# Reordering the first transfers of a two-layer graph network: x of three groups and the 1x1 weights on one queue, the taps' first quarter behind them on two

## The chip, the cores and the metric

The kernel runs on one core of one Trainium2 chip. A core has five engines that run their own instruction streams in order and meet through semaphores: TensorE (PE, matrix products), VectorE (DVE), ScalarE (ACT), GpSimd (POOL) and SyncE (SP, which here does nothing but issue transfers). Transfers (DMAs) can be issued from SyncE, ScalarE and GpSimd; "queue" below means the stream of transfers that one of these engines issues. The metric is the device time of one launch in microseconds; for several runs the median is given.

## The reference

There are 128 graphs of 128 nodes with 256 channels. The part that the change touches is the beginning of layer 0:

```python
h = jnp.maximum(_layernorm(x, axis=-1), 0.0)
...
xc = jnp.transpose(x, (0, 2, 1))          # x is h here
h = _bn(_conv1d(xc, conv1_w, 0), bn1_g, bn1_b, bn1_m, bn1_v)
h = jax.nn.relu(h)
h = _bn(_conv1d(h, conv2_w, 8), bn2_g, bn2_b, bn2_m, bn2_v)
x_conv = jnp.transpose(jax.nn.relu(h + xc), (0, 2, 1))
```

So x is normalized row by row, goes through a 1x1 convolution (`conv1_w`, 256 by 256), a batch norm and a relu, and then through a convolution of 17 taps (`conv2_w`). The rest of layer 0 (an attention-like neighbour product and a gated recurrent unit) and layer 1 (graph convolutions over five groups of nodes) come later and are not touched.

## The kernel before

**Tiles and stages.** x is handled in 32 groups of 4 graphs. Group q sits in the tile `xa` (128 partitions, 4 x 256 values, 512 KB), which has four buffers. `load_x` (lines 357 to 360) fills it with four transfers of 128 KB, each into 32 partitions, all issued from SyncE. `moments` (L267 to L270) takes mean and variance on VectorE and raises the variance to the power -1/2 on GpSimd; `normalize` (L275, VectorE) applies them.

`stage_a` (L367 to L418) then takes a group through PE: transposes to `ph` (L386), a relu to `hTa` on ScalarE (L388), a write of `hTa` to memory from GpSimd (L391), the 1x1 convolution to `pc` (L397), bias and relu to `h` (`h1` in the code; L400 on VectorE, L402 on ScalarE), and a Fourier transform over nodes to `pf` (L408), which is copied to X (L414 or L416). Sixteen groups make a batch; `stage_b` multiplies their spectra by the transformed taps, frequency by frequency.

**The taps.** The taps' transform is made once, beside `stage_a` of the first batch, in four quarters. `load_taps(n, *engines)` (L426 to L433) loads quarter n into one of two buffers of `wt`: four transfers of 256 KB, each into 16 partitions, with transfer r on `engines[r % len(engines)]`, and one of 64 KB (the seventeenth row of each block, L432) on `engines[0]`. `tap_weights` (L435) multiplies them on PE (`pw`, L450), copies the results to `ws` (two buffers; L455, L457) and writes these to memory as `wfd` from GpSimd (L462). Quarters 1 to 3 are loaded from inside `tap_weights` (L441), from SyncE and GpSimd; quarter 0 is loaded ahead of everything.

**Order.** Within one engine, instructions run in the order in which the program states them. That order is made by `Order` and `Lane` (L156 to L204), which interleave the stages by stated costs; it does not depend on how fast transfers are. Ahead of it stands an opening written out by hand (L1099 to L1106): the constants (`cst`, L229) and vectors (`vec`, L231) are issued from ScalarE, then x of group 0, the 1x1 weights `c1w`, x of group 1, the taps' first quarter, x of group 2, and `fold()`.

`fold` (L278 to L302) folds the batch norms into scales: a power on GpSimd (L286), the statistics of group 0 (L287, through `moments`), small VectorE operations (L289 to L291), eight products on PE that spread the scales over columns (`prow`, L297), the normalization of group 0 (L298), and the multiplication of `c1w` by the scales (L301). Then the planned order starts with `stage_a` of three groups at once. On VectorE that puts the statistics of groups 1 and 2 ahead of L400 of group 0, and the statistics of group 3 right before the first tap products are drained.

The opening, as it is before the change:

```python
take_turn("ab", 2)
load_xa(0)
nc.scalar.dma_start(out=c1w, in_=conv1_w.rearrange("(k p) o -> p k o", p=P))
load_xa(1)
load_taps(0, nc.sync, nc.gpsimd, nc.scalar)
load_xa(2)
fold()
```

With three engines given, tap transfers 0 and 3 and the 64 KB one are SyncE's, 1 is GpSimd's and 2 is ScalarE's.

Of the kernel before, what the change touches and what calls it, by code (L numbers as in the profile page):

```python
# [19 lines left out]
P = 128  # L20
# [187 lines left out]
def kernel(ctx: ExitStack, tc: tile.TileContext, x, adj, consts, vecs, w_se, conv1_w,  # L208
                    conv2_w, w_msg, b_msg, w_ih, w_hh, W1, W2, b2, fusion_w, out):
    nc = tc.nc  # L210
# [22 lines left out]
    def c(name):  # L233
        a, b = CAT[name]
        return cst[:, a:b]

    def v(name, i=None):
        a, b = VAT[name]
        return vec[:, a:b] if i is None else vec[:, a + i:a + i + 1]
# [21 lines left out]
    def moments(src, tag):  # L261

        st = f2.tile([P, 4, 6], FP, tag=tag + "st", name="st", bufs=4)
        mv = f2.tile([P, 4, 2], FP, tag=tag + "mv", name="mv", bufs=4)
        rs = f2.tile([P, 4], FP, tag=tag + "rs", name="rs", bufs=4)
        for t in range(4):
            nc.vector.bn_stats(st[:, t], src[:, t])  # L267
            nc.vector.bn_aggr(mv[:, t], st[:, t])
        nc.vector.tensor_scalar(rs, mv[:, :, 1], EPS, None, op0=ALU.add)
        nc.gpsimd.tensor_tensor(rs, rs, c("mhalf")[:, :4], ALU.pow)  # L270
        return mv, rs

    def normalize(dst, src, mv, rs):
        for t in range(4):
            nc.vector.tensor_scalar(dst[:, t], src[:, t], mv[:, t, 0:1], rs[:, t:t + 1],  # L275
                                    op0=ALU.subtract, op1=ALU.mult)

    def fold():  # L278


        s = cp.tile([P, 4], FP, name="s_bn")
        t = cp.tile([P, 4], FP, name="t_bn")
        for i, bn in enumerate(("bn1", "bn2")):
            scl[bn], sft[bn] = s[:, 2 * i:2 * i + 2], t[:, 2 * i:2 * i + 2]
            nc.vector.tensor_scalar(scl[bn], v(bn + "_v"), EPS, None, op0=ALU.add)
        nc.gpsimd.tensor_tensor(s, s, c("mhalf")[:, :4], ALU.pow)  # L286
        MOM[0] = moments(XA[0], "a")  # L287
        for bn in ("bn1", "bn2"):
            nc.vector.tensor_mul(scl[bn], scl[bn], v(bn + "_g"))  # L289
            nc.vector.tensor_mul(sft[bn], v(bn + "_m"), scl[bn])  # L290
            nc.vector.tensor_sub(sft[bn], v(bn + "_b"), sft[bn])  # L291
        prow = ptmp.tile([P, 4, P], FP, tag="tmp", name="prow")
        wide = tw.tile([P, 4, P], FP, tag="wide", name="wide", bufs=1)
        for i, a in enumerate((scl["bn1"][:, 0:1], scl["bn1"][:, 1:2], sft["bn1"][:, 0:1],
                               sft["bn1"][:, 1:2])):
            nc.vector.tensor_copy(wide[:, i], a.to_broadcast([P, P]))
            nc.tensor.matmul(prow[:, i], wide[:, i], ident, start=True, stop=True)  # L297
        normalize(XA[0], XA[0], *MOM[0])  # L298
        nc.vector.tensor_add(brz, v("b_ih")[:, 0:4], v("b_hh")[:, 0:4])
        for k in range(2):  # L300
            nc.vector.tensor_mul(c1w[:, k], c1w[:, k], prow[:, 0:2].rearrange("p a c -> p (a c)"))  # L301
        nc.vector.tensor_copy(brow, prow[:, 2:4].rearrange("p a c -> p (a c)"))  # L302
# [42 lines left out]
    c1w = xf.tile([P, 2, D], FP, name="c1w")  # L345
# [16 lines left out]
    def load_xa(q):  # L362
        if q not in XA:
            XA[q] = LATE["ab"].tile([P, 4, D], FP, tag="xa", name=f"xa{q}", bufs=4)
            load_x(XA[q], q)
# [60 lines left out]
    def load_taps(n, *engines):  # L426

        wt = tw.tile([P, 16, D], FP, tag="wt", name=f"wt{n}")
        src = conv2_w.rearrange("(r n i) t o -> n t r i o", r=4, n=4)[n]
        for r in range(4):  # L430
            engines[r % len(engines)].dma_start(out=wt[32 * r:32 * r + 16], in_=src[:16, r])
        engines[0].dma_start(out=wt[16::32], in_=src[16])  # L432
        wts.append(wt)  # L433
# [665 lines left out]
    order = Order()  # L1099
    take_turn("ab", 2)  # L1100
    load_xa(0)
    nc.scalar.dma_start(out=c1w, in_=conv1_w.rearrange("(k p) o -> p k o", p=P))
    load_xa(1)
    load_taps(0, nc.sync, nc.gpsimd, nc.scalar)
    load_xa(2)
    fold()  # L1106
    beside = Lane([tap_weights()] + [early(q) for q in range(NQ)])
    gates = Lane([fold_gates()], weight=0.5)
# [61 lines left out]
```

## Time and profile before

| What | Value |
|---|---|
| median of three runs | 2103.17 us (2101.92 to 2105.74) |
| the profiled execution | 2104.03 us |
| its span, first to last instruction | 2102.1 us |
| PE busy | 2046.5 us (97%) |
| DVE, POOL, ACT busy | 1180.4 (56%), 723.3 (34%), 687.3 (33%) |
| DMA, first six of 40 slices (52.5 us each) | share 0.9, 0.9, 0.9, 0.7, 0.7, 0.7 |
| moved in these slices | 178, 269, 271, 235, 246, 265 GB/s |
| first matmul | 15.20 us after the span's start |
| first product with taps (L450) | 36.76 us |
| PE busy in 0 to 190 us | 160.84 us |

All times inside an execution are counted from the start of its span. The 1.9 us between the span and the execution's time lie around the first and last instruction. The page's share of busy time is an average over stages, so the opening, one and a half per cent of the span, does not show in it; views cut to the first tens of microseconds do: the chain of waits (what each step was released by, followed back from the end), the timeline, the waits of one engine, and tables of busy time by stretches. A row of such a table has the stretch, its length, busy time of PE, PEld (the loading of weights into PE), DVE, ACT and POOL with the instructions in brackets, PE's granted clock, the DMA share (time that packets took, over 16 engines; it can exceed 1, since packets overlap) and GB/s.

### The profile page before, as it was taken

The numbers are of one execution on the slowest core, as the hardware profiler recorded it, in microseconds if no ns is written. First come the engines' busy times: TensorE is split into PE (matmuls) and PEld (weight loads), VectorE is DVE, ScalarE is ACT, GpSimd is POOL, SyncE is SP. The second block draws the span as 40 slices with busy tenths as digits, with TensorE's granted clock in tenths as the row PEclk, the third lists the DMA queues.
The fourth block names the chain that finished last, engine by engine and source line by source line (L and its number), as shares of the span: only waits on it lengthen the run. The fifth ranks groups of instructions, "written<-read, shape, count | busy, mean of one in ns | idle before, by whom it ended". The sixth has DMA issues, their size and how long they took to land.

```text
span 2102.1 us, 31046 instructions
## 1 busy us (share of the span) xinstructions
PE 2046.5 (97%) x11316; PEld 1656.8 (79%) x11316; DVE 1180.4 (56%) x2775; ACT 687.3 (33%) x1543; POOL 723.3 (34%) x900
## 2 busy tenths in 40 slices
PE   6999999999999999999999999999999999999998
PEld 4667888789888788787778877878787787778875
DVE  5665444786544455645654664566465655654642
ACT  3554222344222333323232232232233323223333
POOL 2443566232565222503332233224323323233230
PEclk9999999999999999999999999999999999999999
DMA  9997778744777634222323332323232333223121
GB/s 178 269 271 235 246 265 263 211 154 151 247 259 258 203 111 141 75 78 73 89 78 86 88 84 71 91 72 87 78 94 73 79 92 92 79 81 99 34 75 51
DMA packets 187050, 281.66 MB, mean 134 GB/s; under 512 B 20685, under 2 KB 140242, under 8 KB 186898
## 3 DMA queue, kind: packets, MB, share of 16 engines
q1 hardware_dynamic: 156066, 184.81, 30.8%
q0 software_dynamic: 30000, 94.13, 13.9%
q8 instruction: 90, 1.47, 0.3%
q10 hardware_dynamic: 832, 0.74, 0.2%
q14 instruction: 62, 0.51, 0.1%
HBM read 187.34 MB, written 92.27 MB: 133 GB/s over the span
## 4 chain that ended last, share of the span: by engine, by line
PE 91%; DMA 3%; DVE 3%; issue 1%; POOL 1%; ACT 0%; SPq 0%; POOLq 0%; DVEq 0%; ACTq 0%
PE p L708 42%; PE pa L501 7%; PE pm L600 5%; PE ph L1030 5%; PE pz L1039 5%; PE pc L397 4%; PE pb L501 3%; PE pi L673 3%; PE px L626 3%; PE pf L408 2%; DMA wfd<-ws 2%; PE pg L1073 1%; PE pc L687 1%; PE po L854 1%; PE ph L386 1%; PE py L1013 1%
## 5 line engine op out<-in xcount | busy, mean ns | idle before, releaser
L834 POOL TENSOR_TENSOR d<-hTc,r 128x512 f32<-128x512 f32 x64 | 81.4, 1273 | 374.1 <-ACT r L831 374.1
L501 PE MATMUL pa<-wf,X 128*128 128x256 f32 x640 | 152.4, 381 | 0.0
L863 POOL DMA_DIRECT2D out<-xt x128 | 71.9, 567 | 206.8 <-DVE xt L860 204.0
L524 DVE SCALAR_TENSOR_TENSOR y<-pa,kk 128x512 f32<-128x512 f32 x78 | 53.8, 690 | 147.4 <-ACT kk L523 147.4
L723 ACT ACTIVATE z<-z,brz 128x256 f32<-128x256 f32 x128 | 58.1, 501 | 225.1 <-DVE z L780 190.9
L708 PE MATMUL p<-th,wrz 128*128 128x256 f32 x512 | 131.6, 379 | 0.0
L708 PE MATMUL p<-tc,wrz 128*128 128x256 f32 x512 | 131.5, 379 | 0.0
L708 PE MATMUL p<-tm,wrz 128*128 128x256 f32 x512 | 131.4, 379 | 0.0
L501 PEld LDWEIGHTS pa<-wf,X 128*128 128x128 f32 x640 | 118.1, 190 | 16.4 <-issue 2.2
L397 PE MATMUL pc<-c1w,hTa 128*128 128x256 f32 x512 | 122.4, 385 | 3.5 <-ACT ef L588 2.3
L600 PE MATMUL pm<-wmsg,hT 128*128 128x256 f32 x512 | 121.7, 382 | 0.0
L690 DVE SCALAR_TENSOR_TENSOR xc<-pc,s_bn,hTc 128x256 f32<-128x256 f32 x128 | 53.1, 476 | 117.4 <-PE pc L687 117.4
L397 PEld LDWEIGHTS pc<-c1w,hTa 128*128 128x128 f32 x512 | 94.1, 192 | 21.6 <-DVE h L400 4.0
L1030 PE MATMUL ph<-yz,w 128*128 128x96 f32 (+3 forms) x640 | 109.0, 324 | 0.9 <-DVE yz L1015 0.9
L600 PEld LDWEIGHTS pm<-wmsg,hT 128*128 128x128 f32 x512 | 95.6, 190 | 16.0 <-issue 1.4
L1032 ACT ACTIVATE hh<-ph,vec 128x96 f32<-128x96 f32 (+3 forms) x160 | 64.2, 403 | 134.0 <-PE ph L1030 124.5
L708 PEld LDWEIGHTS p<-tm,wrz 128*128 128x128 f32 x512 | 97.3, 190 | 13.2
L1039 PE MATMUL pz<-hh,w 128*128 128x96 f32 (+3 forms) x640 | 107.3, 321 | 0.0
L1030 PEld LDWEIGHTS ph<-yz,w 128*128 128x128 f32 x640 | 87.9, 192 | 22.0 <-issue 15.6
L708 PEld LDWEIGHTS p<-tc,wrz 128*128 128x128 f32 x512 | 95.0, 190 | 12.1 <-issue 0.5
L708 PEld LDWEIGHTS p<-th,wrz 128*128 128x128 f32 x512 | 94.7, 190 | 12.3 <-DVE fus L895 0.3
L708 PE MATMUL p<-hTc,wrz 128*128 128x256 f32 x384 | 103.7, 393 | 0.0
(203 smaller groups left out, 4568.8 us busy)
## 6 DMA issues: line engine op xcount, KB each, us to landing
wf<-wfd SPq DMA_DIRECT2D x160, 256.0 KB, 3.9
wfd<-ws POOLq DMA_DIRECT2D x64, 320.0 KB, 7.0
yd<-y POOLq DMA_DIRECT2D x80, 256.0 KB, 3.7
yt<-yd SPq DMA_DIRECT2D x64, 320.0 KB, 4.5
w<-in_W SPq DMA_DIRECT2D x40, 512.0 KB, 3.6
xa<-in_x SPq DMA_DIRECT2D x128, 128.0 KB, 4.9
hTd<-hTa POOLq DMA_DIRECT2D x32, 512.0 KB, 4.6
hT<-hTd SPq DMA_DIRECT2D x32, 512.0 KB
```

What stands on the lines that cost most here:

```text
L397: nc.tensor.matmul(pc[:, i], hT[:, k, (2 * h + i) * N:(2 * h + i + 1) * N], c1w[:, k], start=(k == 0), stop=(k == 1))
L501: nc.tensor.matmul(ps, xk(k), WF[f][:, k, s], start=(k == 0), stop=(k == 1))
L600: nc.tensor.matmul(pm[:, i], hT[:, k, j * N:(j + 1) * N], LATE["wmsg"][:, k], start=(k == 0), stop=(k == 1))
L626: nc.tensor.matmul(px[:, dc, i], msgs[h][:, i, dc * P:(dc + 1) * P], aT[:, 2 * h + i], start=True, stop=True)
L673: nc.tensor.matmul(pi[b * 64:(b + 1) * 64], inv[:F], yt[:, b::2], start=True, stop=True)
L708: nc.tensor.matmul(ps[:, m], w[:, i, k, m * P:(m + 1) * P], factor(i, x, t), start=first and j == 0, stop=last and j == len(n) - 1, skip_g ...
L723: nc.scalar.activation(dst[:, m], src[:, m], AF.Sigmoid, bias=brz[:, b + m:b + m + 1])
L834: nc.gpsimd.tensor_sub(d, hT[:, dc], r[:, dc])
L863: nc.gpsimd.dma_start(out=out[q * GB + j, WIDE:].rearrange("(t n) c -> n t c", n=WIDE), in_=xt[j * WIDE:(j + 1) * WIDE, 1:4])
L1030: nc.tensor.matmul(ph, w1[:, k, m * P:(m + 1) * P], yz[:, k, :, o:o + n], start=(k == 0), stop=(k == 1))
L1032: nc.scalar.activation(hh[:, m], ph, AF.Relu, bias=v("b1", g * 4 + m))
L1039: nc.tensor.matmul(pz, w2[:, g, m, cc * P:(cc + 1) * P], hs[g][:, m], start=(m == 0), stop=(m == 3))
```

## The change

The 1x1 weights are issued from SyncE in place of ScalarE, at the same place among the x loads. The call that loads the taps' first quarter leaves the opening and goes into `fold`, behind the statistics of group 0, and is given two engines: tap transfers 0 and 2 and the 64 KB one are now GpSimd's, 1 and 3 are SyncE's.

```diff
@@ fold()
         nc.gpsimd.tensor_tensor(s, s, c("mhalf")[:, :4], ALU.pow)
         MOM[0] = moments(XA[0], "a")
+        load_taps(0, nc.gpsimd, nc.sync)
         for bn in ("bn1", "bn2"):
@@ the opening
     take_turn("ab", 2)
     load_xa(0)
-    nc.scalar.dma_start(out=c1w, in_=conv1_w.rearrange("(k p) o -> p k o", p=P))
+    nc.sync.dma_start(out=c1w, in_=conv1_w.rearrange("(k p) o -> p k o", p=P))
     load_xa(1)
-    load_taps(0, nc.sync, nc.gpsimd, nc.scalar)
     load_xa(2)
     fold()
```

SyncE's order is thus: group 0 (four transfers), `c1w`, group 1 (four), group 2 (four), taps 1 and 3, and then the x of group 3, which `stage_a` asks for. On GpSimd the three tap issues stand behind the power of L270 for group 0 and ahead of the one for group 1. ScalarE issues nothing more after the constants and vectors. The order of all other instructions on every engine is the same.

## The prediction

> **What bounds the kernel now.** The page's first part has PE busy 97% of the span, so a change at the start matters only if PE is held up there. The chain of waits, cut to 10 to 38 us, shows that it is:
>
> ```profile
> 2.11 9.40 DMA xa<-in_x
> ...
> 15.20 2.08 PE prow L297 x8
> 17.27 1.71 PE ph L386 x8
> 18.98 4.38 PE pc L397 x16
> 23.36 3.77 issue
> 27.13 2.25 PE ph L386 x8
> ```
>
> Columns: start, length, what. Read two holes. PE does nothing until 15.20, because group 0 of x lands at 2.11 + 9.40 = 11.51. Then it stops from 23.36 to 27.13. The chain calls that "issue"; the timeline of 23 to 27.5 us tells more:
>
> ```profile
> 23.69 0.43 DVE L267 BATCH_NORM_STATS2 st<-xa 128x6 f32<-128x256 f32 x1 [2.96 <-DMA xa<-in_x]
> ...
> 25.95 0.17 DVE L269 TENSOR_SCALAR rs<-mv 128x4 f32<-128x4 f32 x1
> 26.03 0.68 DVE L400 TENSOR_TENSOR h<-pc,brow 128x512 f32<-128x512 f32 x1
> ...
> 26.63 1.05 DVE L275 TENSOR_SCALAR xa<-xa,mv,rs 128x256 f32<-128x256 f32 x3
> ```
>
> VectorE executes in order. The statistics of group 2 stand ahead of h (L400) of group 0 and of the normalization (L275) of group 1, which PE's next transposes need. They wait 2.96 us for group 2, which lands at about 23.6. So both holes are late x. Why it is late shows in SyncE's own waits, 0 to 30 us (total, times, longest):
>
> ```profile
> SPq L359 <- DMA c1w<-in_conv_w: 4.6, 1, 4.6
> ...
> SPq L359 <- DMA wt<-in_conv_w: 4.1, 3, 1.7
> SPq L359 <- DMA cst<-in_consts: 2.0, 1, 2.0
> SPq L359 <- DMA vec<-in_vecs: 1.3, 1, 1.3
> ```
>
> An x load waits for the landing of c1w, of taps, of constants: none is its data. It is a limited number of hardware transfers in flight (eight stand issued when SyncE first stops, at 2.56), so what is issued early holds back what follows. The table by stretches has the rate in its last column (the share of DMA time is before it):
>
> ```profile
> 2.50:3.50 1.00, 0.00 (x0) 0.00 (x0) 0.00 (x0) 0.84 (x1) 0.00 (x0) 1.00 1.09 351
> 3.50:7.00 3.50, 0.00 (x0) 0.00 (x0) 0.24 (x2) 0.44 (x1) 0.05 (x1) 1.00 1.01 126
> 7.00:9.00 2.00, 0.00 (x0) 0.00 (x0) 0.00 (x0) 0.00 (x0) 0.98 (x1) 1.00 1.15 230
> 9.00:11.00 2.00, 0.00 (x0) 0.00 (x0) 0.00 (x0) 0.00 (x0) 0.00 (x0) 1.00 1.18 97
> ...
> 21.00:26.00 5.00, 2.35 (x11) 1.71 (x10) 2.13 (x9) 0.00 (x0) 0.82 (x1) 1.00 1.09 214
> 26.00:27.80 1.80, 0.67 (x3) 0.39 (x3) 1.80 (x6) 0.63 (x1) 1.60 (x2) 0.87 0.20 46
> ...
> 40.00:46.00 6.00, 6.00 (x38) 3.53 (x37) 3.97 (x9) 3.05 (x7) 3.22 (x6) 1.00 0.63 188
> ```
>
> With taps in flight the engines are taken up yet move 97 to 131 GB/s (131 in 14 to 19 us); in 21 to 26 us, nearly all x, they move 214. Lastly, does time won at the start last? From 190 us on, PE is busy in 1885.66 of 1912 us, so a shift reaches the end. From 30 to 190 us transfers are dense and PE also waits for ws buffers that writes to wfd still read; there a shift could be given back.
>
> **What the Trainium skill says.** "DMA: Bandwidth & Descriptors", section "Issuing engines are not separate DMA queues": transfers from all issuers share 16 DMA engines; another issuer saves only issue time. So moving c1w from ScalarE to SyncE brings no bandwidth; only the order counts. The trace agrees: the waits above cross queues. "SBUF — State Buffer", section "Door 1: The DMA port swizzle": a transfer's bandwidth depends on how many of 16 ports its partitions reach. By its table one tap transfer (16 partitions) reaches 4, an x transfer (32) reaches 8. The trace agrees in direction (97 to 131 against 214 GB/s), without showing ports. "TensorE: Matmul & The Clock Gate", Part 1: an idle window of about 3.4 us halves the clock. Here 27.8 to 29.6 us has a granted clock of 0.50, after the 3.77 us hole.
>
> **The change, part by part.** L marks the landing of group 0.
>
> 1. Removed from the opening: one tap transfer on GpSimd (issued 1.33), one on ScalarE (2.14); c1w now stands behind group 0 on SyncE. Ahead of L remain constants 188 KB, vectors 24.5 KB, group 0 512 KB: 742 kB. First packets move at about 1.7 us; at 214 GB/s that takes 3.5 us, so 5.2. Another estimate: the last of four issues ends at 2.56, and the x load issued at 29.4 into a nearly empty system landed 2.4 us after its issue. I take L = 5.5. Bounds: 4.8 (the second estimate), and 7.6 (742 kB at 126 GB/s). Gain at L: 11.51 - 5.5 = 6.0.
>
> 2. Group 2 moves ahead of three tap issues on SyncE and behind c1w (one issue, 0.46 us). Bytes up to group 2: 742 + 262 + 1049 = 2053 kB, landing 1.7 + 9.6 = 11.3; at the 167 GB/s that 2 to 27 us averaged, 14.0. VectorE gets to group 2 after group 1: group 1's statistics began 18.32 - 11.51 = 6.8 after L and take 2.4, thus L + 9.2 = 14.7. Group 2 is there in both cases and its wait goes. What is late next is VectorE's own chain: 2.34 us (23.69 to 26.03) of statistics, so L400 starts at L + 11.5 = 17.0 instead of 26.03. Shift there: 9.0 us (6.0 from L, 3.0 from group 2). PE's transposes of group 1 follow at 18.1 instead of 27.13, and the hole shrinks to L + 12.6 less the end of pc at L + 11.85, under 1 us. Clock: the cold stretch may go, yet after 27.13 VectorE sets the pace (L275, then L400 at 29.21), so I count nothing for it.
>
> 3. c1w: landed at 1.65 + 9.9 = 11.55, used by L301 at 17.31 = L + 5.8. Afterwards landed at 1.7 + 1004/214 = 6.4, used at 11.3: hidden, by the statistics. ScalarE loses two issues (0.46 + 0.49), and it is idle until 18.16: nothing.
>
> 4. GpSimd issues three tap transfers (0.69 us was the one at 1.33; about 2 us) behind the power of group 0, which ended at 15.18 = L + 3.7, so 9.2 to 11.2. Behind them waits the power of group 1 (L270), whose input comes at L + 9.2 = 14.7: hidden by 3.5 us; uncovered it would cost 2. hTd of group 0 comes later still.
>
> 5. Taps land later than before in relation to PE. Their first product stood at 36.76, now 27.8; group 3's statistics at 36.61, now 27.6. After group 2 (11.3) there are 1.11 MB of taps and 0.52 MB of group 3 to move: at 146 GB/s (between the 131 and 161 of 14 to 19 and 19 to 21 us) until 22.5. By the longest landing of any tap transfer, 14.0 us, counted from 10.4: 24.4. Hidden by 3 to 5 us.
>
> 6. Backlog. Before, everything up to group 4 (4.17 MB in 2 to 27 us) was in when PE resumed at 27. Now, at 18.1, about 2.05 + 6.8 us x 150 GB/s = 3.1 MB are in; 1.1 MB, or 5.2 us at 214, run into later traffic. Idle DMA time can absorb it: 1.4 us in 26 to 27.8 (share 0.20), 0.7 in 29.6 to 30.4 (share 0.07), 2.2 in 40 to 46 (share 0.63), 4.3 in all. I charge 1.0 us; bounds 0 and 5.2.
>
> Sum: 9.0 - 1.0 = 8.0 us. The profiled execution took 2104.03 (span 2102.1, 1.9 around it): 2096.0. The median of the runs shown, 2103.17, is 0.9 below it: 2095.2.
>
> **Rivals.** (a) The backlog isn't absorbed: the waits for wfd writes, already 3.9 us of PE at 79.8 to 83.65, grow by up to 5.2. For: 60 to 80 us has a DMA share of 1.03. Against: 0.63 in 40 to 46 shows that queues drain. Gain 9.0 - 5.2 = 3.8: 2099.4. (b) More: L = 4.8, no charge, and a cold window fewer at one later wait, where PE works at half speed for 3.4 us, worth 1.7. Gain 9.7 + 1.7 = 11.4: 2091.8. (c) The change doesn't do what it says: the opening is slow by itself, not through taps, and group 0 still lands near 11. For: 97 GB/s at 9 to 11 us with c1w and x in flight too. Against: 351 GB/s at 2.5 to 3.5 before taps piled up. Then group 2 still comes earlier, but behind c1w; gain 0 to 2: 2102. (d) Slower: taps on GpSimd, issued 8 us later, land after PE wants them; PE is in order, so everything behind L450 waits. It costs from 27.8 on, and the kernel is slower from 36.8, 26 us after issue where 14.0 was the longest. Landing at 41: + 4.2, 2107.4.
>
> **How the numbers follow.** Main case 0.60 (2093 to 2098), (a) 0.19, (b) 0.10, (c) 0.05, (d) 0.06. Range 2091 to 2101: it leaves out (c), (d), and the ends of (a) and (b). 0.2%, about what can be told from no change, is 4.2 us, so faster means below 2099.0: main, (b) and a third of (a), 0.76; same: the rest of (a) and (c), 0.18; slower 0.06.
>
> **What would show it.** Group 0's first L267 near 5.6 (now 11.64), L400's first near 17, PE's idle time ahead of group 1's transposes under 1 us, no wait for taps at the first L450 near 28, and the same distance still there at 190 us, where the chain turns to PE. I am wrong if L267 starts after 8, if PE waits at L450, or if the shift of 9 us near 27 has shrunk below 5 by 190.

## The result and the profile after

| | before | after |
|---|---|---|
| median of 20 runs each | 2104.34 us (2101.11 to 2112.02) | 2096.78 us (2094.63 to 2103.97) |
| profiled execution, its span | 2104.03, 2102.1 us | 2096.45, 2094.4 us |
| PE busy | 2046.5 us | 2042.4 us |
| group 0 of x lands | 11.51 us | 6.39 us |
| first h of group 0 (L400, now L401) | 26.03 us | 17.95 us |
| transposes of group 1 on PE | 27.13 us | 19.06 us |
| first product with taps | 36.76 us | 28.68 us |

The ratio is 0.9965, with an interval of 0.9957 to 0.9973: faster, by 7.6 us between the medians and 7.6 us between the profiled executions. From line 288 to the opening the line numbers are one higher than before.

First the chain of waits of the kernel after, cut to 0 to 26 us (start, length, what):

```profile
2.11 4.28 DMA xa<-in_x
...
10.07 2.09 PE prow L298 x8
...
18.05 0.59 DVE h L401
18.64 2.58 DVE xa L275 x8
...
23.02 2.05 PE pc L398 x8
```

The first wait is for the same transfer as before, the last of group 0, but 4.28 us long in place of 9.40: L, the landing of group 0, is 2.11 + 4.28 = 6.39. `prow` moves with it. The piece of "issue" of 3.77 us is gone; in its place the chain runs through VectorE, from h of group 0 to the normalization of group 1.

The timeline of the kernel after, cut to the instructions that the forecast named (start, length, engine, line, operation; in brackets the idle time before it):

```profile
6.51 0.43 DVE L267 BATCH_NORM_STATS2 st<-xa 128x6 f32<-128x256 f32 x1 [0.95 <-DMA xa<-in_x]
...
15.61 0.43 DVE L267 BATCH_NORM_STATS2 st<-xa 128x6 f32<-128x256 f32 x1
15.69 1.03 POOL L270 TENSOR_TENSOR rs<-rs,cst 128x4 f32<-128x4 f32 x1 [3.75 <-DVE rs L269]
...
17.95 0.68 DVE L401 TENSOR_TENSOR h<-pc,brow 128x512 f32<-128x512 f32 x1
...
19.06 1.69 PE L387 MATMUL ph<-cst,xa 128*128 128x128 f32 x8 [0.55 <-PE pc L398]
...
28.68 1.10 PE L451 MATMUL pw<-wt,cst 17*80 17x512 f32 x8
```

The line at 15.61 is group 2. It has no bracket: VectorE goes straight from group 1's statistics to group 2's, where it stood 2.96 us before. GpSimd has idled 3.75 us when the power of group 1 comes up, so the tap issues that now stand ahead of it (9.99 to 11.94) were done in time. PE's hole ahead of the transposes of group 1 is 0.55 us. The first product with taps has no bracket either: the taps are there.

SyncE's waits of the kernel after, 0 to 30 us (total, times, longest):

```profile
SPq L360 <- DMA xa<-in_x: 4.3, 5, 3.2
...
SPq L360 <- DMA wt<-in_conv_w: 1.5, 1, 1.5
...
SPq L360 <- DMA c1w<-in_conv_w: 0.6, 1, 0.6
```

The wait of an x load for c1w has shrunk from 4.6 to 0.6 us, those for taps from 4.1 to 1.5. What is left are mostly waits of x for earlier x, and for the release of a buffer of x (3.7 us for PE, 3.4 for VectorE; not shown).

And the table by stretches of the kernel after (DMA share and GB/s are the last two columns):

```profile
2.50:3.50 1.00, 0.00 (x0) 0.00 (x0) 0.00 (x0) 0.44 (x1) 0.00 (x0) 1.00 1.06 329
3.50:7.00 3.50, 0.00 (x0) 0.00 (x0) 0.69 (x4) 0.00 (x0) 1.03 (x1) 1.00 1.12 226
7.00:9.00 2.00, 0.00 (x0) 0.00 (x0) 1.86 (x9) 0.00 (x0) 0.00 (x0) 1.00 1.15 215
9.00:11.00 2.00, 0.93 (x4) 0.93 (x5) 1.86 (x11) 0.00 (x0) 1.98 (x3) 1.00 1.15 221
...
14.00:19.00 5.00, 4.51 (x16) 3.26 (x15) 4.68 (x19) 0.82 (x2) 1.91 (x2) 1.00 1.15 157
```

SyncE issues its two tap transfers at 8.0 to 9.0, behind the x of three groups, and GpSimd its three at 9.99 to 11.94. From 3.5 to 11 us the rate stays at 215 to 226 GB/s; before it was 126 in 3.5 to 7 and 97 in 9 to 11. In 14 to 19, with all taps issued, it drops to 157. The DMA engines are equally taken up in both.

What becomes of the shift later? Both traces hold the same PE instructions, so the start of one can be subtracted from the start of the other. `pse` below are products of a later stage, which read `hT` back from memory:

```
PE instruction                       before    after   earlier by
transposes of group 1                 27.13    19.06     8.07
first product with taps               36.76    28.68     8.08
product behind a wait for ws          83.65    76.81     6.84
first pse (hT read back)             184.17   180.81     3.36
190 us of the kernel after                               6.3
430 to 700 us                                            4.7
from 910 us on                                           8.0
```

So the shift isn't kept as it is: part is given back between 71 and 184 us and near 391 us, and some returns near 190, 867 and 908 us. That is what the forecast's last step was about, and most experiments are about it.

### The profile page after: what moved, and what is told of

It is laid out like the page before. It is cut to its first block, busy times and chain, and to the rows that moved or that the text cites. A ratio compares the mean times of both kernels' runs of the same rounds, so it can differ in the third digit from the quotient of the medians.

```text
span 2094.4 us, 31048 instructions
## 1 busy us (share of the span) xinstructions
PE 2042.4 (98%) x11316; PEld 1653.2 (79%) x11316; DVE 1180.7 (56%) x2775; ACT 687.3 (33%) x1543; POOL 726.1 (35%) x902
## 4 chain that ended last, share of the span: by engine, by line
PE 91%; DVE 4%; DMA 3%; issue 1%; POOL 1%; ACT 1%; SPq 0%; POOLq 0%; DVEq 0%; ACTq 0%
PE p L709 42%; PE pa L502 7%; PE pm L601 5%; PE ph L1031 5%; PE pz L1040 5%; PE pc L398 4%; PE pb L502 3%; PE pi L674 3%; PE px L627 3%; PE pf L409 2%; PE pg L1074 1%; DMA xa<-in_x 1%; DMA wfd<-ws 1%; PE po L855 1%; PE pc L688 1%; PE ph L387 1%
```

## The experiments

The kernels before and after were also profiled again beside the experiments, to see how much two executions of one program differ.

**Group 2 ahead of the taps, nothing else.** From the kernel before:

```diff
     load_xa(1)
-    load_taps(0, nc.sync, nc.gpsimd, nc.scalar)
     load_xa(2)
+    load_taps(0, nc.sync, nc.gpsimd, nc.scalar)
     fold()
```

> The kernel before with one line moved: the taps' first quarter is issued behind group 2 in the opening, still from three engines, so that one tap transfer on GpSimd and one on ScalarE stay ahead of group 0. By the forecast (two separate gains: taps out of group 0's way, group 2 out of the taps' way) only the second is had: first statistics stay near 11.6, the first L400 comes at about 23 in place of 26.0, and the kernel is 2 to 3 us faster than before (ratio 0.9987). A rival, that group 2's place is the whole effect: L400 near 18, 7 to 8 us faster. Another, that neither matters without the other: no change.

Measured: 2103.99 us beside 2106.02, ratio 0.9989 (0.9980 to 0.9997). Its timeline:

```profile
11.28 0.43 DVE L267 BATCH_NORM_STATS2 st<-xa 128x6 f32<-128x256 f32 x1 [4.86 <-DMA xa<-in_x]
...
22.73 0.68 DVE L400 TENSOR_TENSOR h<-pc,brow 128x512 f32<-128x512 f32 x1
```

Group 0 is as late as before (11.28; before 11.64), yet h comes 3.3 us earlier, and so do PE's transposes (23.84). So group 2's order among SyncE's loads is worth about 3 us in the opening by itself. What is left of the 8.1 us is the earlier landing of group 0, 5.1 us; that part was not tried without the other.

**c1w.** Two runs: the kernel after with c1w back on ScalarE, whose edit is shown, and the kernel before with c1w moved to SyncE, at the same place.

```diff
-    nc.sync.dma_start(out=c1w, in_=conv1_w.rearrange("(k p) o -> p k o", p=P))
+    nc.scalar.dma_start(out=c1w, in_=conv1_w.rearrange("(k p) o -> p k o", p=P))
```

> The changed kernel with the 1x1 weights issued from ScalarE again, beside group 0. By the forecast the transfers share the same engines, so 262 kB more stand ahead of group 0's landing, 1.2 us at 214 GB/s: first statistics at 7.7 in place of 6.5, first tap product near 29.9, and still 6 to 7 us faster than before. The rival, that moving these weights to SyncE's queue is what frees group 0: first statistics at 9.5 or later, less than 5 us faster.

> The kernel before with only the 1x1 weights moved to SyncE, the taps left where they were. By the forecast two tap transfers still run beside group 0, so it lands 0 to 1.2 us earlier (first statistics at 10.4 to 11.6), group 2 stays behind the taps, and the kernel is 0 to 1.5 us faster (ratio 0.9993 to 1). By the rival (the weights' queue is the cause) 4 us or more.

Measured: on ScalarE in the new order 2099.05 us, ratio to before 0.9971 (0.9962 to 0.9980); on SyncE in the old order 2106.61, ratio 1.0001 (0.9990 to 1.0012). The first statistics, from the timelines of the first and of the second:

```profile
7.24 0.43 DVE L267 BATCH_NORM_STATS2 st<-xa 128x6 f32<-128x256 f32 x1 [1.84 <-DMA xa<-in_x]
```

```profile
12.00 0.43 DVE L267 BATCH_NORM_STATS2 st<-xa 128x6 f32<-128x256 f32 x1 [5.91 <-DMA xa<-in_x]
```

In the old order the move does nothing that can be told from chance (statistics at 12.00, where 10.4 to 11.6 was expected and the kernel before has 11.64; L400 at 25.61, before 26.03; time unchanged). In the new one it is worth 0.7 us at group 0 (7.24 against 6.51; 1.2 was expected): ScalarE issues c1w at 1.65, ahead of group 0's last transfer, and SyncE at 2.59, behind it. The total doesn't resolve that: the two intervals overlap. That it is the order that acts, and not the engine that issues, fits both runs.

**Does a tap transfer slow group 0 by its bytes or by its shape?** Two kernels, each the kernel after with 256 KB more ahead of group 0, issued from GpSimd: one tap transfer into 16 partitions, or c1w into 128. In the first, `load_taps` then uses this tile and leaves this transfer out (not shown).

```diff
     take_turn("ab", 2)
+    WT0 = [tw.tile([P, 16, D], FP, tag="wt", name="wt0")]
+    nc.gpsimd.dma_start(out=WT0[0][32:48],
+                        in_=conv2_w.rearrange("(r n i) t o -> n t r i o", r=4, n=4)[0][:16, 1])
     load_xa(0)
...
```

```diff
     take_turn("ab", 2)
+    nc.gpsimd.dma_start(out=c1w, in_=conv1_w.rearrange("(k p) o -> p k o", p=P))
     load_xa(0)
-    nc.sync.dma_start(out=c1w, in_=conv1_w.rearrange("(k p) o -> p k o", p=P))
     load_xa(1)
```

> The changed kernel with one of the four tap transfers (256 KB into 16 partitions) issued from GpSimd at the very start, as in the kernel before. By the forecast (tap transfers are slow for their size) group 0 lands 1.2 us later for the bytes and 1 to 2 us more: first statistics at 8.7 to 9.7 in place of 6.5. If only bytes count, at 7.7.

> The changed kernel with the 1x1 weights issued from GpSimd at the very start, where the kernel before issues a tap transfer: the same 256 KB from the same issuer at the same time, but into 128 partitions in place of 16. If a tap transfer's shape is what slows the opening, first statistics come at 7.3 to 7.9 (1.2 us for the bytes at 214 GB/s), well ahead of the 9.29 that the tap transfer gave. If any early transfer from GpSimd does it, at about 9.3.

The first statistics and the stretch of 3.5 to 7 us, first with the tap transfer (the timeline, then the table):

```profile
9.29 0.43 DVE L267 BATCH_NORM_STATS2 st<-xa 128x6 f32<-128x256 f32 x1 [2.55 <-DMA xa<-in_x]
```

```profile
3.50:7.00 3.50, 0.00 (x0) 0.00 (x0) 0.24 (x2) 0.00 (x0) 0.17 (x1) 1.00 1.08 126
```

then with c1w:

```profile
7.61 0.43 DVE L267 BATCH_NORM_STATS2 st<-xa 128x6 f32<-128x256 f32 x1 [2.10 <-DMA xa<-in_x]
```

```profile
3.50:7.00 3.50, 0.00 (x0) 0.00 (x0) 0.24 (x2) 0.00 (x0) 1.03 (x1) 1.00 1.12 226
```

The same 256 KB from the same engine cost group 0 1.1 us (7.61 - 6.51) in 128 partitions and 2.8 us (9.29 - 6.51) in 16. One tap transfer alone brings the rate back to the 126 GB/s of the kernel before, and costs 2.8 of the 5.1 us. So it is the shape, and not the bytes. Both transfers move in 64 packets of 4 KB; in these traces a packet of the tap transfer takes 0.53 us on the mean, one of c1w 0.27, and between 3.5 and 7 us a packet of x (1 KB) takes 0.135 beside the one and 0.083 beside the other. What of the shape does it was not tried apart: a tap transfer puts sixteen rows into each of its partitions and c1w two, and a partition's rows stand 17 KB apart in memory in the one and 128 KB in the other. Each kernel has one execution (2098.79 and 2097.18 us), too little to tell their totals apart.

**Is the shift given back because more bytes are left over?** The kernel after with a copy of 1.05 MB within device memory (into a new tile `spare`), issued from SyncE behind the taps; nothing reads the copy. That doubles the backlog that the forecast counted (1.1 MB).

```diff
         load_taps(0, nc.gpsimd, nc.sync)
+        nc.sync.dma_start(out=spare, in_=x[64:72].rearrange("b n c -> (b n c)")
+                          .rearrange("(p f) -> p f", p=P))
```

> The changed kernel with 1.05 MB more to move in the opening: a copy from memory to memory, issued from SyncE behind the two tap transfers and ahead of group 3, read by nobody. If bytes left over from the opening are what delays the writes of ws later (backlog), this doubles them: the stretch from group 1's transposes to 190 us grows by 2 to 5 us against the changed kernel. If the later waits are made by what is issued at that time, it stays within 1.5 us, and group 3 lands some 5 to 8 us later without anybody waiting.

Measured: 2093.68 us in the one run, 2106.65 for the kernel before beside it. PE's timeline, the transposes of group 1 and the two waits that gave back the shift:

```profile
18.93 2.09 PE L389 MATMUL ph<-cst,xa 128*128 128x128 f32 x8 [1.40 <-issue]
...
75.24 2.49 PE L453 MATMUL pw<-wt,cst 17*80 17x512 f32 x8 [3.44 <-ACT ws L458]
...
176.52 0.64 PE L583 MATMUL pse<-hT,wse 128*32 128x128 f32 x16 [1.24 <-DMA hT<-hTd]
```

The extra megabyte lengthened neither wait: from the transposes to pse it took 157.6 us, and 161.8 in the kernel after without it. Group 3's first transfer landed at 23.63 in place of 17.17, and nothing waited for it. In its first 40 us this kernel moved 9.2 MB (229 GB/s), the kernel after 7.9 (198 GB/s), so the copy was through long before the two waits. It is one execution, but rival (a) had the wait for ws grow by up to 5.2 us with left-over bytes, and with twice as many it is 3.44, as before the change.

**How much do these waits vary in one program?** The kernel before once more, and the kernel after a second and a third time.

> The kernel before once more, for a second profile. By the forecast's backlog step, the stretch from the transposes of group 1 to the first spectra products is as long as in the first profile (165 to 167 us from 27.1). If that stretch differs by 2 us or more between two profiles of the same kernel, what the changed kernel seemed to give back there (2.2 us) can't be told from chance.

> The changed kernel once more. First statistics at 6.3 to 6.8, first tap product at 28.5 to 29.2 by every theory. By the backlog step the stretch from there to 190 us is again about 2 us longer than in the kernel before; by chance it varies by as much.

> The changed kernel as it is, for the same chip and runs as the two versions above and for a third profile of it: first statistics at 6.3 to 6.8, ratio 0.9957 to 0.9973.

PE's timelines at the two waits, before, before again, after, after again, after a third time:

```profile
83.65 2.49 PE L450 MATMUL pw<-wt,cst 17*80 17x512 f32 x8 [3.88 <-ACT ws L455]
...
184.17 0.64 PE L580 MATMUL pse<-hT,wse 128*32 128x128 f32 x16 [0.37 <-DMA hT<-hTd]
```

```profile
83.74 2.45 PE L450 MATMUL pw<-wt,cst 17*80 17x512 f32 x8 [3.14 <-ACT ws L455]
...
187.27 0.65 PE L580 MATMUL pse<-hT,wse 128*32 128x128 f32 x16 [2.36 <-DMA hT<-hTd]
```

```profile
76.81 2.49 PE L451 MATMUL pw<-wt,cst 17*80 17x512 f32 x8 [5.11 <-ACT ws L456]
...
180.81 0.64 PE L581 MATMUL pse<-hT,wse 128*32 128x128 f32 x16 [2.90 <-DMA hT<-hTd]
```

```profile
76.56 2.49 PE L451 MATMUL pw<-wt,cst 17*80 17x512 f32 x8 [4.68 <-ACT ws L456]
...
181.84 1.08 PE L581 MATMUL pse<-hT,wse 128*32 128x128 f32 x16 [5.27 <-DMA hT<-hTd]
```

```profile
75.62 2.49 PE L451 MATMUL pw<-wt,cst 17*80 17x512 f32 x8 [4.06 <-ACT ws L456]
...
181.78 1.08 PE L581 MATMUL pse<-hT,wse 128*32 128x128 f32 x16 [5.71 <-DMA hT<-hTd]
```

At pse the kernel before stands at 184.17 and 187.27, mean 185.7; after at 180.81, 181.84 and 181.78, mean 181.5. So 4.2 us of the 8.1 are left there, with single pairs from 2.3 to 6.5. The wait for ws is longer after (4.1 to 5.1 us, before 3.1 and 3.9), that for hT too. But from the transposes of group 1 to pse the two profiles of before take 157.0 and 160.4 us, 3.4 apart, more than the 2 us that the expectation named as the limit for telling a loss from chance. And in the two edits of the kernel before (taps behind group 2; c1w on SyncE) the wait for hT is 3.4 and 2.7 us, in six edits of the kernel after 1.2 to 4.1, and in a seventh, the last below, 7.4. That the new order lengthens this wait is not shown. The third profile of after took 2104.9 us, the slowest of its seven runs (median 2098.92, ratio 0.9962, 0.9945 to 0.9978): one pair of profiles can't price what happens past 70 us; the medians can.

**Can the give-back be had?** Three kernels. The first issues the late part of the constants at the end of the taps' transform, not in its second quarter. The second does the same, and also splits the first load of constants at column `CNOW`, so that only what `fold` and the first transposes use is ahead of group 0. The third is the second with group 2's statistics moved later in the planned order, behind the first h.

```diff
-                if (n, m) == (1, 3):
+                if (n, m) == (3, 3):
                     load_late()
```

> The changed kernel with the two late loads (embedding weights and the second part of the constants, 0.54 MB, issued near 63 us) moved from the second to the last quarter of the taps. If what was given back between 70 and 125 us is bytes queued ahead of the writes of ws, 0.54 MB less is worth up to 2.5 us at 214 GB/s: PE's stall at 71.7 us (5.1 us) shrinks to 2.6 to 4, and the kernel is 1 to 3 us faster than the changed one. If it is a matter of which transfers meet by chance, the stall is as long as before or moves, and the time is that of the changed kernel within 1 us.

```diff
-    nc.scalar.dma_start(out=cst[:, :CFIRST], in_=consts[:, :CFIRST])
+    nc.scalar.dma_start(out=cst[:, :CNOW], in_=consts[:, :CNOW])
...
     load_xa(1)
+    nc.sync.dma_start(out=cst[:, CNOW:CFIRST], in_=consts[:, CNOW:CFIRST])
     load_xa(2)
```

> The changed kernel with the late loads in the last quarter of the taps, as before in this study, and with two thirds of the first constants (123 kB of Fourier and tap tables, first used 20 us in) taken from ahead of group 0 to behind group 1. Group 0 lands 0.5 us earlier: first statistics at 5.8 to 6.2, first tap product near 28.2. PE's stall near 72 us stays at 2 to 3.5. The kernel is 0.5 to 3 us faster than the changed one (ratio to before 0.9953 to 0.9963).

```diff
         if q not in MOM:
+            if q == 2:
+                yield 0.0, 4.5
             MOM[q] = moments(XA[q], "a")
```

> The same with the planner told to start group 2's statistics 4.5 us later in its own time, which puts them behind h of group 0 and the normalization of group 1 on VectorE. If VectorE's order is now what holds PE between groups 0 and 1, L400's first comes 1.5 to 2.4 us earlier than in the kernel without it (near 15.5 to 16) and the first tap product 1 to 2 us earlier. If it only moves the wait to group 2, the first tap product stays where it was.

The first: 2097.59 us, ratio 0.9961 (0.9946 to 0.9976). Its wait for ws was 2.38 us, a little under the 2.6 to 4 that was expected, but that for hT 4.08: the total can't be told from the kernel after. The second: 2096.93 us, ratio 0.9950 (0.9936 to 0.9964), the best of all, but its interval overlaps that of the change. Group 0's statistics start at 6.07 and the first tap product at 28.25, both 0.4 us earlier than after.

The third is slower than the kernel before: 2110.6 us, ratio 1.0024 (1.0014 to 1.0033), though its first h and its first tap product (25.80) come earlier than in any other kernel. VectorE's and PE's timelines of it, then its chain of waits, 55 to 80 us:

```profile
73.49 0.43 DVE L268 BATCH_NORM_STATS2 st<-xa 128x6 f32<-128x256 f32 x1 [8.48 <-DMA xa<-in_x]
```

```profile
77.23 2.50 PE L412 MATMUL pf<-cst,h 128*128 128x160 f32 x8 [12.28 <-ACT h L406]
```

```profile
65.00 8.37 DMA xa<-in_x
...
75.93 0.60 DVE h L404
...
76.55 0.64 ACT h L406
...
77.23 2.50 PE pf L412 x8
```

It is the same pattern as in the kernel before, sixty microseconds later. Statistics of a later group wait 8.48 us for their x, with h of an earlier group behind them on VectorE, and PE waits 12.28 us for that h. The x was issued only at 65.0: SyncE had stood 20.6 us at a tap load, for a buffer that PE had not yet released (15.4 us in the kernel after). Moving one step in the plan moved others relative to their loads; the expectation had only the opening in view, and there the gain came (first h at 15.32).

## Why the prediction was right, step by step

The forecast was 2095.2 us; the median is 2096.8, inside its main case.

1. *L.* The mechanism holds: taps ahead of group 0 were what made it late, and with them gone the stretch to 7 us runs at 226 GB/s. The term was mis-sized: 742 kB at 214 GB/s gave 5.2, 5.5 was taken, and L was 6.39. The gain is 5.1 us in place of 6.0. The rate was not the error: from 1.7 to 6.39 us the trace moves 225 GB/s. But that is 1.06 MB in place of 742 kB. SyncE's queue alone moved 0.84 MB, and group 0 is 0.52 of it: the other 0.3 MB are c1w and x of group 1, issued from 2.59 us on. What stands behind group 0 in the queue still took rate from it. (The sum's lower bound is also off: 2.56 + 2.4 is 5.0, not 4.8.)

2. *Group 2.* As forecast, its wait goes and VectorE's own chain sets h. From the landing of group 0 to h it took 17.95 - 6.39 = 11.6 us (forecast 11.5). The second gain was put at 3.0 us; it is 3.0 here (8.1 less 5.1), and 3.3 where it was tried alone. The hole was put under 1 us, and is 0.55. The stretch at half clock near 28 is gone (1.00), and in this pair that is worth nothing, as the forecast had it: the shift is 8.07 us ahead of it and 8.08 behind. In the second profile of before the stretch was twice as long, and its loss is worth 1.1.

3. *c1w.* Hidden as forecast, and its new queue alone is worth nothing. In the new order, leaving it on ScalarE costs 0.7 us at group 0; the forecast had this inside L, as bytes that no longer stand ahead of group 0. The waits across queues, which the forecast took as a sign that issuers share the DMA engines, show only a limit on transfers in flight (eight are issued when SyncE first stops, before and after). That another issuer brings nothing is shown by the run with c1w moved alone.

4. *GpSimd.* Cover of 3.5 us forecast ahead of group 1's power, 3.75 measured.

5. *Taps.* No wait at the first product at 28.68, none for group 3. GpSimd's tap transfers landed 10.8 to 13.7 us after issue, within the 14.0 that was taken as the worst. Rival (d) is out.

6. *Backlog.* The charge of 1.0 us came out near the net: 8.1 us at 28.7 became 7.6 us at the end. But that is luck. What the step described, left-over bytes that run into later traffic, isn't what the runs show: a megabyte more cost nothing. They show a shift of 8.1 that is 4.2 on the mean at pse, through longer waits for ws and hT. The text said it would be wrong if the shift fell below 5 by 190, and by this sign the step was wrong more often than right. Two profiles of before and three of after make six pairs. At 190 us of the kernel after they stand at 3.7, 3.9, 4.3, 4.8, 5.9 and 6.3, 4.8 on the mean.

What happens behind that can be read from the first pair. From 190 us on its shift changes for good in three steps, and each falls on a stretch at half clock that one trace has and the other hasn't: from 6.3 to 4.7 at 391 us (a stretch of after), to 6.3 at 867 and to 8.0 at 908 (stretches of before). The table by stretches has the last two, before and then after (the clock is the third column from the end):

```profile
860.00:915.00 55.00, 52.38 (x243) 42.57 (x242) 34.73 (x90) 13.83 (x31) 19.70 (x29) 0.94 0.25 66
```

```profile
860.00:915.00 55.00, 52.38 (x251) 41.26 (x251) 30.67 (x79) 16.16 (x36) 17.64 (x25) 1.00 0.26 71
```

PE is as busy in both, but 0.06 of 55 us is 3.3 us at full speed, and 3.3 us is what the shift gains here. In other pairs such stretches fall otherwise: at the end the six stand between -0.8 and 10.5 us, 5.3 on the mean. So the profiles don't price the change; the medians do, with 7.6.

How much of the 7.6 is a better clock can only be estimated. Within the 20 runs of after (mean granted clock 0.9904) a clock higher by 0.001 goes with 1.3 us less. Seven later runs of after had 0.9907 and the 19 of before beside them 0.9888: that would be 2.5 us. The forecast counted nothing for the clock in its main case and 1.7 us for one cold window fewer in rival (b). What stays open is which meeting of transfers makes the waits for ws and hT long in one execution and short in another.

Rival (c), an opening that is slow by itself, is out: group 0 came 5.1 us earlier.

## What to carry to other kernels

Ask of each load in an opening not when its own data is used but what it holds back: here both holes of PE in the opening were waits for x behind taps that nothing needed until 36.76 us, and ordering the loads by first use closed them. Price a transfer beside a critical one by its shape and not only by its bytes: here 256 KB into 16 partitions delayed group 0 by 2.8 us, and into 128 by 1.1. And count what is issued behind a load as well, if it is issued before the load has landed. And when one wait in an in-order engine goes, check the next load that the same engine will meet: the kernel with the earliest first product was the only one that measured clearly slower than before.

## What the runs showed of the hardware that was not expected

*The time of one program scatters with the granted clock.* The 20 runs of after lie within 2094.6 to 2104.0 us, a scatter larger than the change itself. It goes with the mean granted clock (correlation -0.84 over 20 runs). The first and the third profile of after (2096.45 and 2104.9 us) show how: the same PE instructions lie 0.6 us apart at 870 us and 8.7 at 2085, and the distance grows at stretches at half clock that the third has and the first hasn't, by 3.3 us at 874, 1.4 at 905, 1.7 at 1060 and 1.7 at 1298 (one of the first at 1883 and one of the third at 2031 cancel). PE's timelines at the first of them, in the first profile and in the third:

```profile
871.88 0.70 PE L709 MATMUL p<-xm,wn 128*128 128x256 f32 x2 [1.80 <-DVE r L825]
...
872.94 1.94 PE L674 MATMUL pi<-yt,cst 80*64 80x512 f32 x8
```

```profile
872.52 0.70 PE L709 MATMUL p<-xm,wn 128*128 128x256 f32 x2 [1.80 <-DVE r L825]
...
873.58 2.98 PE L674 MATMUL pi<-yt,cst 80*64 80x512 f32 x8
```

Both waited 1.80 us. In the first execution the next eight products take 1.94 us, in the second 2.98. The tables by stretches, again the first and then the third:

```profile
872.80:876.20 3.40, 3.40 (x15) 1.73 (x15) 0.42 (x1) 1.97 (x4) 3.00 (x3) 1.00 0.65 195
```

```profile
872.80:876.20 3.40, 3.40 (x12) 0.98 (x11) 0.42 (x1) 2.04 (x3) 2.43 (x2) 0.72 0.51 154
876.20:879.60 3.40, 3.40 (x9) 2.52 (x8) 0.00 (x0) 0.60 (x1) 3.24 (x4) 0.50 0.71 190
```

Such stretches last 3.41 us or multiples of it (3.41, 6.83 and 10.24 in the profiles of before and after), on a grid of their own: in the first profile of before they begin at 27.3, 81.9, 191.2 and 382.3 us, and the later three stand 16, 48 and 104 times 3.413 us behind the first. The Trainium skill, "TensorE: Matmul & The Clock Gate", Part 1, describes a free-running window of 3413 ns; the traces agree in length and grid. Its table has the clock halved after at least one idle window of that length; here a half clock began 1.8 us after a wait of only 1.80 us in one execution, and not at all after the same wait in the other. What decides between the two isn't shown.

*A tap transfer took the rate from 226 to 126 GB/s* for everything beside it, with nearly equally busy DMA engines (share 1.08 against 1.12). The direction was in the forecast; that a single transfer of 256 KB suffices was not. So the busy share doesn't show here what such a transfer costs; its packets do.
